# A softplus step with a PSUM operand, its product with x on GpSimd, and new durations in a list scheduler

## The chip, the cores and the metric

The kernel runs on one core of a Trainium2 chip, as one launch. The metric is the device time of that launch in microseconds; lower is better. The core has five engines that run their own instruction queues in order and wait for one another by semaphores: TensorE (matmuls and transposes, PE in the profile, with its weight loads as PEld), VectorE (DVE), ScalarE (ACT), GpSimd (POOL) and SyncE (SP), which here issues nearly all DMAs.

## The reference

Four layers follow one another on an image batch of 8 x 256 x 32 x 32 in float32. Layer 0 is an attention block with a depthwise position term and a feed-forward block with an 8 x 8 Fourier filter; layer 1 is another attention block with group norms; layer 2 is a chain of quantized convolutions that ends in codes of 0 to 255. Layer 3 runs a Mamba block over each image in four directions. The part of it that the change touches is the step size `dt`, which is a softplus, and its product with the convolved and gated input x:

```python
x = jax.nn.silu(xc).swapaxes(1, 2)
x_dbl = x @ W_x.T
dt = jax.nn.softplus(x_dbl[..., :DT_RANK] @ W_dt.T + b_dt)
Bm = x_dbl[..., DT_RANK:DT_RANK + D_STATE]
Cm = x_dbl[..., DT_RANK + D_STATE:]
A = -jnp.exp(A_log)
# for every position of the sequence:
dA = jnp.exp(dt_t[:, :, None] * A)
h = h * dA + dt_t[:, :, None] * B_t[:, None, :] * u_t[:, :, None]
y = jnp.einsum('bdn,bn->bd', h, C_t)
```

There are 512 inner channels, 16 states for each, and 1024 positions; `dt * u` is the product that the change moves.

## The kernel before, in words

**Two phases.** `phase_a` computes layers 0 to 2 for the eight images, each as a strand of generator functions, and stores the codes in DRAM. `phase_b` is the Mamba phase. It goes over 8 images x 4 directions x 2 halves of 512 positions: 64 blocks. A block is 16 groups, one for each state; a group has four channel tiles of 128 channels.

**The order of the work.** Nothing is put in order by hand. Every operation is an `_Op` with an engine and a cost, an estimate of its duration. `_Order.run` is a list scheduler that runs while the program is built: each strand offers its next operation (or list of operations), `start` works out when it could begin from the costs of what has been placed, with 0.35 us for a step from one engine to another, and the one that can begin first is emitted, ties going to the lower rank. So the costs set the order in which each engine's queue is filled; on the chip every queue then runs in that order, and an instruction that has to wait holds up all that is behind it. A strand may give its own cost with a list, as in `yield (SCORES, ops)`. All of the instructions are emitted from one line, L134, which is why the profile's groups are told apart by tiles.

**Fillers.** In `phase_a`, when the list has TensorE idle before an operation, `fill` emits matmuls of a constant into a spare bank (L1077 in the profile), one for each 0.3 us of the planned gap.

**Rooms.** A `_Room` is a set of buffers; `take` waits until one is free and `put` gives it back. Those that matter here, all of `[128, 512]` float32: `dt` (8), `tmp` (3), `xs` (11), `da` (5), `h` (6 pairs) in SBUF, and in PSUM `py` (4 banks, the sums over the states), `db` (3 banks, the scan's input) and `pp`, a single bank. `lend` hands out `pp` to everything beside the scan's own stream: the input projections, the convolution (`conv`), `xdbl`, the softplus steps, the transposes of `du`, the `fold` and the outputs. (Until the first block's softplus steps are done it lends the `py` banks.)

**One group's stream.** ScalarE scales the transposed product by a state's B (`dbu`), TensorE transposes the result into a `db` bank, ScalarE makes the decay `da` as an exponential, VectorE scans (`h`), ScalarE copies the last column (`st`), GpSimd multiplies a pair of scan outputs by C in place (`h<-h,cb`), and TensorE transposes that into the `py` banks, where the sixteen states add up.

**The softplus step.** `steps(n)` makes four strands `dt(c)`, one for each channel tile, which are started during the block before. With v the matmul's result in `pp`, a step computes t = exp(-|v|) on ScalarE, o = max(v, 0) + t on VectorE, then u1 = (t + 1) - 1 on VectorE and ln(1 + t) on ScalarE, and o - u1 + ln(1 + t) on GpSimd. Subtracting (t + 1) - 1 takes back the t that was added with the rounding that 1 + t has. Then o * x goes to u1 on VectorE, TensorE transposes it into `pp` in four pieces, and VectorE copies that to `duT`. The bank `pp` is given back right after o = max(v, 0) + t, and taken anew for the transposes.

Of the kernel before, what the change touches and what calls it, by code (L numbers as in the profile page):

```python
# [20 lines left out]
F32 = mybir.dt.float32  # L21
# [8 lines left out]
P = 128  # L30
# [67 lines left out]
class _Op:  # L98


    def __init__(self, engine, method, args, kw):
        self.engine, self.method, self.args, self.kw = engine, method, args, kw
        out, ins = args[0], [a for a in (*args[1:], *kw.values()) if isinstance(a, bass.AP)]
        self.reads = {k for a in ins for k in self.blocks(a)}
        self.writes = {k for a in (out, kw.get("accum_out")) if a is not None for k in self.blocks(a)}
        self.landing = 0.0
        n = max(math.prod(a.shape[1:]) for a in (out, *ins)) / 1024
        near = all(a.space == out.space and out.space != PSUM for a in ins)
        if engine == "tensor":
            x = kw.get("rhs", ins[0])  # L110
            n = math.prod(x.shape[1:]) / 1024
            move = method == "transpose" or kw.get("is_transpose", False)
            self.cost = max(0.06, n * (0.93 if move else 0.44 if x.dtype != F32 else 1.76 if n > 0.2 else 2.1))
        elif engine == "vector":
            fast = near and method in ("tensor_scalar", "tensor_copy")
            both = near and method == "tensor_tensor"
            scan = method == "tensor_tensor_scan"
            self.cost = 0.04 + n * (2.2 if scan else 0.57 if fast else 1.1) + (0.3 if fast or both else 0)
        elif engine == "scalar":
            self.cost = 0.05 + 0.87 * n + (0.1 if len(ins) > 1 else 0)  # L120
        elif engine == "gpsimd":
            self.cost = 0.13 + 2.17 * n if method == "tensor_tensor" else 0.3 + n
        else:
            self.cost, self.landing = 0.1, 3.0

# [28 lines left out]
class _Room:  # L154
# [6 lines left out]
    def take(self, shape=None, dtype=None):  # L161
        k = self.left.pop(0)
        t = self.pool.tile(shape or self.shape, dtype or self.dtype, name=f"{self.tag}{k}", tag=f"{self.tag}{k}")
        self.of[t.name] = k
        return t

    def put(self, t):
        self.left.append(self.of.pop(t.name))


class _Order:
# [7 lines left out]
    def __init__(self, nc):  # L179
        self.nc, self.strands, self.n = nc, [], 0  # L180
        self.free, self.written, self.read, self.base, self.last = {}, {}, {}, {}, {}
        self.fill = None

    def add(self, rank, strand):
        self.n += 1
# [4 lines left out]
    def go(self, s, value=None):  # L190
        try:
            r = s[1].send(value)
            if isinstance(r, _Op):
                r = (r.cost, [r])
            elif isinstance(r, list):
                r = (sum(o.cost for o in r), r)
            s[2] = r
        except StopIteration:
            self.strands.remove(s)
# [63 lines left out]
def phase_a(ctx, tc, i, col, ident, codes, w_parts):  # L263
# [268 lines left out]
    def maxima(rank, q, k, rows, done):  # L532

        both = yield from take(stats)
        least, sums = both[:, 0], both[:, 1]
        todo = [(t, j, h) for t in range(NT) for j in range(2) for h in (0, 2)]
        left = [MAXIMA]

        def some():
            while todo:  # L540
                yield lambda: not todo or may(2)
                if not todo:
                    break
                n = 4 if may(4) and not todo[0][2] else 2
                t, j, h = todo.pop(0)
                if n == 4 and todo:
                    todo.pop(0)
                bb = yield from some_banks(n)
                ops = []
                for e in range(n):  # L550
                    r = slice(32 * (h + e), 32 * (h + e) + 32)
                    ops.append(
                        T.matmul(bb[e], lhsT=q[r, t * P : (t + 1) * P], rhs=k[r, hs(j)], start=True, stop=True)
                    )
                yield (0.9 if n == 2 else 1.0, ops)
                for e in range(n):
                    m, s = (x[:, j, t, h + e : h + e + 1] for x in (least, sums))
                    yield V.tensor_reduce(m, bb[e], AX.X, ALU.max, negate=True)
                    yield A.activation(bb[e], bb[e], AF.Exp, bias=m, accum_out=s)
                    back(bb[e])  # L560
            left[0] -= 1

        for _ in range(MAXIMA):
            order.add((1, rank), some())
        yield lambda: left[0] == 0 and not making
        making.append(1)
        m, mx, t = (small.tile([P, NT, 4], F32, name=f"mx{e}", tag=f"mx{e}", bufs=2) for e in range(3))
        yield V.tensor_tensor(m, least[:, 0], least[:, 1], ALU.min)
        for j in range(2):
            yield V.tensor_tensor(least[:, j], m, least[:, j], ALU.subtract)  # L570
        yield A.activation(least, least, AF.Exp)
        yield V.tensor_tensor(sums, sums, least, ALU.mult)
        yield V.tensor_tensor(t, sums[:, 0], sums[:, 1], ALU.add)

        y = small.tile([P, NT, 4], F32, name="ln", tag="ln", bufs=2)
        put(stats, both)
        yield A.activation(y, t, AF.Ln)
        yield V.tensor_tensor(mx, y, m, ALU.subtract)
        yield A.activation(y, y, AF.Exp, scale=-1.0)
        yield V.tensor_tensor(t, t, y, ALU.mult)  # L580
        yield V.scalar_tensor_tensor(mx, t, -1.0, mx, ALU.add, ALU.add)
        for e in range(2):
            b = small.tile([P, NT, 4], BF16, name="mb", tag="mb", bufs=2)
            yield V.tensor_copy(b, mx)
            yield V.tensor_copy(parts[:, :, :, e], b)
            yield V.tensor_tensor(mx, mx, parts[:, :, :, e], ALU.subtract)
        yield V.tensor_copy(parts[:, :, :, 2], mx)
        for h in range(2):
            pr = yield from side()
            yield [  # L590
                T.transpose(pr[:, t * P : (t + 1) * P], parts[:, 4 * h + t].rearrange("p a b -> p (a b)"), ident)
                for t in range(4)
            ]
            yield A.copy(rows[:, hs(h)], pr)
            back(pr)
        making.clear()
        done()

    def exponentials(rank, tasks, vt, n, finish):
# [5 lines left out]
        for task, (h, steps) in enumerate(tasks):  # L605
# [31 lines left out]
            def values(k, four, tiles, po=po, seen=seen, last=len(steps) - 1):  # L637
                es = [t[:, e] for t in tiles for e in range(2)]
                yield lambda: seen[0] == k
                ops = []  # L640
                for e, (q, kk, rows, key, r, c, at) in zip(es, four):
                    ops.append(
                        T.matmul(
                            po[at : at + n], lhsT=vt[:, key, c : c + n], rhs=e,
                            start=(k == 0 and key == 0), stop=(k == last), skip_group_check=True,
                        )
                    )
                yield (0.9 * (4 * n // P), ops)
                for t in tiles:
                    put(exps, t)  # L650
                seen[0] += 1
# [403 lines left out]
    def fill(gap, ops):  # L1055
# [6 lines left out]
            [order.last.get((bank.tag, k), 0.0) for k in bank.left] + [order.base.get(o.args[0].name, 0.0)] * own,  # L1062
            default=1e9,
        )
        n = int((gap - max(free, since)) / FILL)
        if n < 1:
            return
        if spare is not None and order.last.get((bank.tag, spare), 0.0) <= since:
# [9 lines left out]
        if t is not None:  # L1078
            bank.put(t)

    order.fill = fill
    stage = [0] * B

    def sample(b):
# [53 lines left out]
def phase_b(ctx, tc, i, col, ident, codes, w_parts, out):  # L1138
# [186 lines left out]
    def steps(n):  # L1325
# [6 lines left out]
        def dt(c):  # L1332
# [1 line left out]
            if c == 0:  # L1334
                d.duT[h] = yield from take(du_room)
            o = yield from take(dt_room)
            t, u1 = yield from takes(2, tmp_room)
            room, ps = yield from lend()
            yield T.matmul(ps, lhsT=w_dt[2 * DS :, c * P : (c + 1) * P], rhs=xd[2 * DS :], start=True, stop=True)
            left[0] -= 1  # L1340
# [4 lines left out]
            yield A.activation(t, ps, AF.Abs)  # L1345
            yield A.activation(t, t, AF.Exp, scale=-1.0)
            yield V.scalar_tensor_tensor(o, ps, 0.0, t, ALU.max, ALU.add)
            put(room, ps)
            yield V.tensor_scalar(u1, t, 1.0, -1.0, ALU.add, ALU.add)
            yield A.activation(t, t, AF.Ln, bias=1.0)  # L1350
            yield G.tensor_tensor(o, o, u1, ALU.subtract)
            yield G.tensor_tensor(o, o, t, ALU.add)
            put(tmp_room, t)
            d.dt[c, h] = o
            yield V.tensor_tensor(u1, o, d.xs[c, h], ALU.mult)
            yield lambda: h in d.duT
            room, pt = yield from lend()
            yield [T.transpose(pt[:, t * P : (t + 1) * P], u1[:, t * P : (t + 1) * P], ident) for t in range(TH)]
            put(tmp_room, u1)
            yield V.tensor_copy(d.duT[h][:, :, c * P : (c + 1) * P], pt.rearrange("p (t k) -> p t k", t=TH))  # L1360
            put(room, pt)
            done.add(("du", c))
# [385 lines left out]
```

## Time and profile before

| | us |
|---|---|
| median of 3 runs | 10703.6 (10692.3 to 10710.17) |
| the profiled execution, its own time | 10710.81 |
| its span, first to last instruction | 10708.9 |
| PE busy | 9899.2 (92%) |
| DVE busy | 8487.3 (79%) |
| ACT busy | 8702.0 (81%) |
| POOL busy | 6736.6 (63%) |

The span lies 1.9 us below the time of the same execution, and that execution 7 us above the median. Busy shares are those of the whole span; the profile's slices show that the first third or so (layers 0 to 2) loads VectorE and GpSimd far less than the Mamba phase does, so each phase has to be read from a window of its own. A row of a group gives the engine, the operation, the tiles written and read, the shapes and the count, then busy time in us, the mean of one in ns, the engine's idle time just before these instructions, and what ended most of it. TensorE's busy time is that of pipelined matmuls with modelled ends and is no measure of work done.

### The profile page before, as it was taken

How to read it: one execution, taken by the hardware profiler on the slowest of the kernel's cores; microseconds unless marked ns; L12 is line 12 of the kernel's file. 1: busy time of each engine (PE TensorE's matmuls, PEld its weight loads, DVE VectorE, ACT ScalarE, POOL GpSimd, SP SyncE). 2: the span in 40 equal slices, each digit the busy share in tenths (PEclk: the TensorE clock that was granted, in tenths of full speed). 3: DMA queues.
4: the chain of work that ended last, by engine and by line, in shares of the span. 5: the costliest groups of instructions: out<-in, count | busy, mean ns of one | idle time of the engine just before them, and what ended most of it. 6: DMA issues, size and time to landing. Idle time of an engine off the chain costs nothing. (4 is left out here: it accounts for less than half of the span.)

```text
span 10708.9 us, 157325 instructions
## 1 busy us (share of the span) xinstructions
PE 9899.2 (92%) x58614; PEld 6251.0 (58%) x58726; DVE 8487.3 (79%) x8991; ACT 8702.0 (81%) x16284; POOL 6736.6 (63%) x3746
## 2 busy tenths in 40 slices
PE   9999999999999899899999999999989999998998
PEld 3333323333333267777777777777777777777776
DVE  5456657577675389888998998998899899899898
ACT  7867676777767488888888988888888888888988
POOL 1532133132220178888888888888888888888888
PEclk8998998999989899999999999999999999999999
DMA  1100000000000011111111111111111111111111
GB/s 53 32 18 16 22 17 22 13 22 13 14 13 10 20 46 41 48 52 47 47 46 52 50 42 56 41 49 52 45 48 52 47 47 46 51 50 43 56 40 50
DMA packets 217346, 410.01 MB, mean 38 GB/s; under 512 B 24881, under 2 KB 69297, under 8 KB 211458
## 3 DMA queue, kind: packets, MB, share of 16 engines
q1 hardware_dynamic: 216578, 399.94, 12.5%
q8 instruction: 461, 7.55, 0.3%
q14 instruction: 307, 2.51, 0.1%
HBM read 358.43 MB, written 30.93 MB: 36 GB/s over the span
## 5 line engine op out<-in xcount | busy, mean ns | idle before, releaser
L134 POOL TENSOR_TENSOR h<-h,cb 128x1024 f32<-128x1024 f32 x2048 | 4874.1, 2394 | 917.3 <-ACT st L134 462.7
L134 ACT ACTIVATE da<-dt,am 128x512 f32<-128x512 f32 x4096 | 2884.7, 717 | 515.6 <-DVE h L134 509.3
L134 DVE TENSOR_TENSOR_SCAN h<-da,st,db 128x512 f32<-128x512 f32 x2048 | 2469.2, 1260 | 177.2 <-PE db L134 96.9
L134 DVE TENSOR_TENSOR_SCAN h<-da,db 128x512 f32<-128x512 f32 x2048 | 2346.4, 1199 | 240.4 <-PE db L134 158.7
L134 ACT ACTIVATE dbu<-du,bT 128x512 f32<-128x512 f32 x3584 | 2487.7, 714 | 30.5 <-PE db L134 28.1
L134 PE MATMUL db<-ident,dbu 128*128 128x128 f32 x14336 | 2218.5, 280 | 169.1 <-DVE h L134 139.6
L134 PE MATMUL py<-ident,h 128*128 128x128 f32 x16384 | 2122.2, 275 | 91.5 <-POOL h L134 83.6
L134 PEld LDWEIGHTS db<-ident,dbu 128*128 128x128 f32 x14336 | 1669.9, 143 | 704.9 <-DVE h L134 377.9
L134 PEld LDWEIGHTS py<-ident,h 128*128 128x128 f32 x16384 | 1843.7, 142 | 168.4 <-POOL h L134 134.0
L134 DVE TENSOR_REDUCE stats<-bank 128x1 f32<-128x512 f32 x1536 | 983.0, 684 | 742.8 <-PE bank L134 741.3
L134 ACT ACTIVATE bank<-bank,stats 128x512 f32<-128x512 f32 x1536 | 1024.5, 672 | 380.9 <-DVE stats L134 370.4
L134 POOL TENSOR_TENSOR mid<-mid,mid 128x961 f32<-128x961 f32 (+2 forms) x192 | 400.3, 2092 | 1056.2 <-ACT mid L134 714.9
L134 PE MATMUL bank<-big,big 32*128 32x512 f32 x4096 | 913.3, 674 | 38.0 <-ACT bank L134 18.7
L134 PE MATMUL pp<-xi,cvd 128*128 128x512 f32 x2016 | 930.6, 605 | 3.5 <-DVE dt L134 1.5
L134 ACT ACTIVATE exps<-bank 128x512 f32<-128x512 f32 x1536 | 797.5, 620 | 135.6 <-PE bank L134 131.2
L134 PE MATMUL db<-dg,du 128*128 128x128 f32 x4096 | 809.0, 280 | 0.0
L134 DVE TENSOR_TENSOR tmp<-dt,xs 128x512 f32<-128x512 f32 x256 | 599.3, 2341 | 173.3 <-POOL dt L134 172.6
L134 POOL TENSOR_TENSOR dt<-dt,tmp 128x512 f32<-128x512 f32 x512 | 653.1, 1276 | 122.6 <-DVE tmp L134 97.5
L134 PEld LDWEIGHTS db<-dg,du 128*128 128x128 f32 x4096 | 636.2, 196 | 0.0
L134 DVE SCALAR_TENSOR_TENSOR mid<-mid,cols,mid 128x961 f32<-128x961 f32 (+1 forms) x384 | 597.2, 1555 | 6.9
L134 PEld LDWEIGHTS pp<-xi,cvd 128*128 128x128 f32 x2016 | 371.9, 195 | 384.3 <-issue 374.2
L134 PEld LDWEIGHTS bank<-big,big 32*128 32x128 f32 x4096 | 285.5, 193 | 503.2 <-issue 253.9
(212 smaller groups left out, 11329.5 us busy)
## 6 DMA issues: line engine op xcount, KB each, us to landing
cb<-c_d SPq DMA_DIRECT2D x1024, 256.0 KB, 3.2
wi<-w_in SPq DMA_DIRECT2D x192, 192.0 KB, 3.5
big<-in_x_dram SPq DMA_DIRECT2D x16, 1024.0 KB, 5.4
kept<-big SPq DMA_DIRECT2D x16, 1024.0 KB, 4.0
big<-kept SPq DMA_DIRECT2D x16, 1024.0 KB, 4.8
cdb<-codes SPq DMA_DIRECT2D x48, 256.0 KB, 4.2
big<-big SPq DMA_DIRECT2D x16, 512.0 KB, 6.7
out_dram<-z SPq DMA_DIRECT2D x32, 256.0 KB, 2.7
```

The source lines that it names most:

```text
L134: return getattr(getattr(nc, self.engine), self.method)(*self.args, **self.kw)
```

## The change

The first part is in the softplus step. The first product of the step, (t + 1) - 1, is written into the PSUM bank that held the matmul's result, VectorE subtracts it from o, and the bank is given back after that. GpSimd only adds ln(1 + t), and it now also does the product with x, into the temporary t; the second temporary u1 is gone.

The second part is in the list scheduler's durations. A matmul whose moving data has fewer than 20 rows costs 0.22 more, a ScalarE operation with a second operand read from memory 0.13 more in place of 0.1, a `tensor_tensor` on GpSimd 0.17 + 2.17 n in place of 0.13 + 2.17 n (n in units of 1024 elements). In `phase_a` alone, every list of TensorE operations without a cost of its own gets 0.1 more (`way`), the list of matmuls in `maxima` is 1.06 whether it has two or four, those of `values` 0.88 for each 128 output rows and 0.12, and `fill` takes 0.35 us off a gap before it counts fillers. In `phase_b` `way` stays at 0.

```diff
-            self.cost = max(0.06, n * (0.93 if move else 0.44 if x.dtype != F32 else 1.76 if n > 0.2 else 2.1))
+            self.cost = max(0.06, (0.22 if x.shape[0] < 20 else 0) + n * (0.93 if move else 0.44 if x.dtype != F32 else 1.76 if n > 0.2 else 2.1))
...
-            self.cost = 0.05 + 0.87 * n + (0.1 if len(ins) > 1 else 0)
+            self.cost = 0.05 + 0.87 * n + (0.13 if len(ins) > 1 else 0)
         elif engine == "gpsimd":
-            self.cost = 0.13 + 2.17 * n if method == "tensor_tensor" else 0.3 + n
+            self.cost = 0.17 + 2.17 * n if method == "tensor_tensor" else 0.3 + n
...
-        self.fill = None
+        self.fill, self.way = None, 0.0
...
-                r = (sum(o.cost for o in r), r)
+                r = (sum(o.cost for o in r) + self.way * (r[0].engine == "tensor"), r)
...
-                yield (0.9 if n == 2 else 1.0, ops)
+                yield (1.06, ops)
...
-                yield (0.9 * (4 * n // P), ops)
+                yield (0.88 * (4 * n // P) + 0.12, ops)
...
-        n = int((gap - max(free, since)) / FILL)
+        n = int((gap - max(free, since) - 0.35) / FILL)
...
-    order.fill = fill
+    order.fill, order.way = fill, 0.1
...
-            t, u1 = yield from takes(2, tmp_room)
+            t = yield from take(tmp_room)
...
             yield V.scalar_tensor_tensor(o, ps, 0.0, t, ALU.max, ALU.add)
+            yield V.tensor_scalar(ps, t, 1.0, -1.0, ALU.add, ALU.add)
+            yield A.activation(t, t, AF.Ln, bias=1.0)
+            yield V.tensor_tensor(o, o, ps, ALU.subtract)
             put(room, ps)
-            yield V.tensor_scalar(u1, t, 1.0, -1.0, ALU.add, ALU.add)
-            yield A.activation(t, t, AF.Ln, bias=1.0)
-            yield G.tensor_tensor(o, o, u1, ALU.subtract)
             yield G.tensor_tensor(o, o, t, ALU.add)
-            put(tmp_room, t)
             d.dt[c, h] = o
-            yield V.tensor_tensor(u1, o, d.xs[c, h], ALU.mult)
+            yield G.tensor_tensor(t, o, d.xs[c, h], ALU.mult)
             yield lambda: h in d.duT
             room, pt = yield from lend()
-            yield [T.transpose(pt[:, t * P : (t + 1) * P], u1[:, t * P : (t + 1) * P], ident) for t in range(TH)]
-            put(tmp_room, u1)
+            yield [T.transpose(pt[:, k * P : (k + 1) * P], t[:, k * P : (k + 1) * P], ident) for k in range(TH)]
+            put(tmp_room, t)
```

## The prediction

> **What bounds the kernel now.** I read the busy shares first, then the scan stretch alone as one window, then the waits in it, then the tile that the change touches. The page's slices show two stages: attention and convolution up to some 3700 us, then the Mamba phase, in which all four engines show 8 or 9 tenths. The window from the first scan to the last (columns: PE, PEld, DVE, ACT, POOL busy):
>
> ```profile
> 3747.00:10663.00 6916.00, 6330.26 (x42789) 4956.78 (x42896) 6223.37 (x5647) 6029.42 (x10493) 5813.06 (x3235) 0.98 0.16 48
> ```
>
> TensorE is busy 91.5%, VectorE 90.0%, ScalarE 87.2%, GpSimd 84.1% of it: no engine is far ahead, so no engine's saved time comes through whole. The waits between 3800 and 10600 us say who holds the others up:
>
> ```profile
> ACT da L134 <- DVE h L134: 501.0, 470, 5.7
> POOL h L134 <- ACT st L134: 437.5, 311, 5.4
> PEld db L134 <- DVE h L134: 370.6, 723, 2.4
> POOL h L134 <- DVE h L134: 268.2, 309, 3.0
> ...
> PE pp L134 <- DVE tmp L134: 195.7, 146, 2.1
> DVE tmp L134 <- POOL dt L134: 170.2, 109, 3.0
> ```
>
> ScalarE waits for scans to give back decay tiles, weight loads wait for scans to give back PSUM banks, GpSimd waits for scan outputs: VectorE is what the rest is late for. VectorE in turn stands 170 us before one instruction, the product with x, and TensorE stands 196 us before the transposes of that product, with all later matmuls queued behind. The tile's own view and the groups show why (minimum/median/maximum ns; busy us, mean ns):
>
> ```profile
> L134 POOL TENSOR_TENSOR dt<-dt,tmp x512: 1262/1274/1645, 3723.7 to 10531.2; 128x512 f32<-128x512 f32 x171
> L134 DVE TENSOR_SCALAR tmp<-tmp x256: 409/694/2589, 3723.2 to 10525.2; 128x512 f32<-128x512 f32 x128
> L134 DVE TENSOR_TENSOR tmp<-dt,xs x256: 660/2599/2852, 3726.7 to 10532.7; 128x512 f32<-128x512 f32 x128
> ...
> L134 DVE TENSOR_TENSOR tmp<-dt,xs 128x512 f32<-128x512 f32 x256 | 599.3, 2341 | 173.3 <-POOL dt L134 172.6
> L134 DVE TENSOR_SCALAR tmp<-tmp 128x512 f32<-128x512 f32 x256 | 289.5, 1131 | 0.1
> L134 DVE TENSOR_TENSOR yT<-py,yT 128x512 f32<-128x512 f32 x64 | 40.2, 672 | 3.6 <-PE py L134 3.6
> ```
>
> The same shape of product takes 660 ns at best and 2599 ns at the median, and the timeline shows what it does in between:
>
> ```profile
> 7015.85 2.35 POOL L134 TENSOR_TENSOR h<-h,cb 128x1024 f32<-128x1024 f32 x1
> ...
> 7015.93 2.83 DVE L134 TENSOR_TENSOR tmp<-dt,xs 128x512 f32<-128x512 f32 x1 [1.90 <-POOL dt L134]
> ```
>
> GpSimd's product began 0.08 us earlier and ended at 7018.20; VectorE's ended at 7018.76, 0.56 us after it. Most of the 2.83 us is standing still.
>
> [...] The trace agrees for a PSUM source (the add of py and yT, 672 ns, never stretched by GpSimd); a PSUM destination from an SBUF source isn't in it.
>
> **The change part by part**, for 256 softplus steps (64 blocks x 4 channel tiles).
>
> *VectorE.* Out go the product (256 x 2341 ns = 599 us) and (t+1)-1 in SBUF (256 x 1131 ns = 290 us), 889 us. In come (t+1)-1 written to the PSUM bank and the subtraction that reads it. For the second I take the 672 ns of the py add. The first is not in the trace: its bounds are 409 ns (the unblocked SBUF form) and 733 ns (the xi scaling from PSUM); I take 0.69 us. 256 x (0.67+0.69) = 348 us. Net 541 us less VectorE work, and the 170 us of standing before the product go too.
>
> *GpSimd.* The subtraction leaves (256 x 1276 ns), the product arrives at the same shape and 1276 ns: zero net. No longer blocked by VectorE's two operations, its long products, 2394 ns mean against 2342 at best, may return up to 2048 x 0.05 = 100 us, on an engine 84% busy; I count none.
>
> *ScalarE, TensorE, DMA.* The same instructions, counts and shapes; no DMA and no queue of SP or POOL issues is touched. The product's transposes read the other temporary. One temporary a step instead of two leaves more of the three free.
>
> *The bank.* All this side work goes through one PSUM bank, pp. Following it in the trace from first matmul to last reader, it is occupied some 4440 us, 64% of the stretch; a softplus step holds it 4.2 us. Now it is given back only after the subtraction: 0.69 + 0.67 us more, and one scan more (1.26 us mean of a scan with carry) where the list puts one while ScalarE takes the logarithm: 1.4 to 2.6 us. 256 x 2.6 = 670 us, occupancy at most 74%. What waits for it is the next matmul into pp, mostly the convolution's, and behind that in TensorE's queue the db and py transposes. I cost it at nothing: the list knows of the hold and puts transposes ahead. If that cover goes, it is the slow rival below.
>
> *What reaches the end in the Mamba phase.* VectorE falls from 90% to (6223-541)/6916 = 82%; TensorE at 91.5% is next, so the gain is what TensorE's idle time of 6916-6330 = 586 us gives back. Of it 196 us is before the product's transposes: the list plans 0.89 us for a product that takes 2.34, so TensorE comes early. On GpSimd the plan (0.17+1.09 = 1.26) meets the 1.28 measured; I give back three quarters, 147 us, the rest being steps where GpSimd is itself late. Before db transposes with scans as cause:
>
> ```profile
> L134 PE MATMUL db<-ident,dbu 128*128 128x128 f32 x14078 | 2178.3, 280 | 165.8 <-DVE h L134 137.3 <-ACT dbu L134 7.3
> ```
>
> Half of 137 us, 69. Before the fold's transposes 28 us wait for VectorE's ys; half, 14. Sum **230 us**, 3.6 us a block of 108.
>
> *The durations.* In the Mamba phase the list gets 0.03 us more for a ScalarE operation with a tile as scale, 0.04 more on GpSimd's products, 0.22 more for the matmul of 17 rows; nothing is added to the machine, orders shift, and I price that inside the 230. In the first phase the new terms move each list of matmuls by about 0.1 us and take 0.35 us off each gap before filler matmuls are counted:
>
> ```profile
> L1077 PE MATMUL bank<-minus 128*128 128x512 bf16 (+1 forms) x1622 | 475.7, 416 | 43.2 <-ACT bank L134 33.9 <-ACT exps L134 6.0 <-POOL eps L316 1.6
> ```
>
> 1622 fillers stand in 445 bursts, 134 of them single. 0.35/0.3 = 1.17 fewer each: 134 + 311 x 1.17 = 498 fewer, at 475.7/1622 = 0.293 us some 146 us of TensorE time. In the attention rounds I read, ScalarE's work (four exponentials, 2.06 us, and two accumulating ones with their reads, 1.8) fills the 3.88 us round, so a filler there hides behind ScalarE. I count a fifth, **30 us**. Bounds: 146 us gained at best; 60 us lost if the new order fits worse or the clock, 0.92 here, falls with fewer fillers (2% of 3300 us).
>
> Against the profiled execution: 10708.9 us span, 10710.8 its own time, 7 us above the median of 10703.6. 10710.8 - 230 - 30 = 10451; set off from the median, **10444 us**.
>
> **The rivals.**
>
> *VectorE's whole gain comes through.* For it: nearly every large wait names VectorE. Against: TensorE 91.5%. If ScalarE (6029 us) then runs at 95%, the stretch is 6029/0.95 = 6346 us, 570 less: with the 30, 10104. Part of the way, 10200. Chance 0.12.
>
> *Nothing moves.* The transposes wait for GpSimd's product as they did for VectorE's, and TensorE's order sets the pace; only the first phase changes: 10690. [...] Chance 0.04.
>
> *Slower: the pp bank blocks TensorE's queue.* The step's hold grows by 2.6 us; in 78% of the steps the next matmul into the bank came within 2 us of the release in the trace. If the list's order doesn't cover it, each step stalls TensorE by 2.6 - 0.9 = 1.7 us: 256 x 1.7 = 435 us, against 260 gained: 10880. It decides where the new stall passes 260/256 = 1.0 us a step. Against it: 36% of the stretch leaves the bank free, and a delayed side job has half a block before it is needed. Chance 0.12.
>
> *As forecast*: chance 0.72, its own range 10310 to 10570.
>
> **How the numbers follow.** The range takes the forecast's range on to half of the large gain and to small gains that the bounds of the PSUM form (256 x 0.3 = 70 us) and of the first phase leave: 10210 to 10670. A measurement here can tell about 0.2%, 21 us. Faster: 0.72 + 0.12 plus a little of the second rival, 0.85; same 0.03; slower 0.12.
>
> **What would show it.** Right: no VectorE row for the product; the PSUM forms near 0.7 us without stretched ones; GpSimd's product at 1.28 us; VectorE near 82% of the stretch; ScalarE's wait for scans well under 501 us; TensorE's wait before the product's transposes near 50 us; some 1100 fillers. Wrong: waits of TensorE for pp's subtraction of over 250 us, transposes waiting for GpSimd's product as long as now, or a first phase more than 60 us longer.

## The result and the profile after

The changed kernel takes **10383.5 us** (median of 4 runs, 10378.2 to 10388.1) against 10706.9 us before: a ratio of 0.9702 with a 95% interval of 0.9687 to 0.9718, 323 us less. The forecast was 10444 us with a range of 10210 to 10670, so the measured time lies inside it and 60 us below the forecast. The first scan starts at 3702 us in place of 3747, the scans take 6639 us in place of 6915, and what follows them 44 in place of 46: 45, 276 and 2 us.

The window from the first scan to the last, of the kernel after (columns as before: PE, PEld, DVE, ACT, POOL busy, then the granted clock):

```profile
3702.00:10341.00 6639.00, 6270.11 (x42898) 4912.56 (x42896) 5716.34 (x5647) 6006.93 (x10493) 5729.03 (x3235) 0.99 0.17 50
```

VectorE's busy time has fallen by 507 us. TensorE, at 94.4%, is the busiest, with ScalarE next at 90.5%; TensorE's idle time went from 586 to 369 us and its busy time from 6330 to 6270. The two add up to the 277 us.

The changed operations in the view of the tile tmp, after (minimum/median/maximum ns):

```profile
L134 POOL TENSOR_TENSOR tmp<-dt,xs x256: 1263/1275/1292, 3683.4 to 10210.7; 128x512 f32<-128x512 f32 x128
...
L134 DVE TENSOR_SCALAR pp<-tmp x252: 694/695/697, 3737.9 to 10206.8; 128x512 f32<-128x512 f32 x126
```

Neither is stretched: the PSUM form spans 3 ns between its fastest and its slowest, where its SBUF form went from 409 to 2589. TensorE's groups in the scan window, with the idle time before them and its causes; two of them before the change:

```profile
L134 PE MATMUL pp<-xi,cvd 128*128 128x512 f32 x2008 | 925.0, 604 | 3.5 <-DVE dt L134 1.5 <-DVE du L134 0.9
...
L134 PE MATMUL pp<-ident,tmp 128*128 128x128 f32 x1008 | 158.8, 280 | 226.9 <-DVE tmp L134 195.7 <-ACT xs L134 15.0 <-ACT dbu L134 9.9
```

and after it:

```profile
L134 PE MATMUL db<-ident,dbu 128*128 128x128 f32 x14334 | 2199.0, 278 | 194.8 <-DVE h L134 168.5 <-ACT dbu L134 10.7
...
L134 PE MATMUL pp<-xi,cvd 128*128 128x512 f32 x2008 | 948.2, 616 | 24.3 <-DVE dt L134 23.8
...
L134 PE MATMUL pp<-ident,tmp 128*128 128x128 f32 x1008 | 154.3, 276 | 17.7 <-ACT xs L134 9.5 <-DVE ys L134 4.1 <-POOL tmp L134 4.1
```

The 227 us before the product's transposes are down to 18. Before the convolution's matmuls TensorE now stands 24 us in place of 3.5, with VectorE's subtraction, which frees the bank, as cause. VectorE's own waits for TensorE, before the change (3800 to 10600 us):

```profile
DVE h L134 <- PE db L134: 242.7, 149, 4.3
...
DVE h L134 <- PE py L134: 70.4, 53, 7.5
```

The waits of the kernel after, 3600 to 10300 us:

```profile
PEld db L134 <- DVE h L134: 414.3, 698, 2.7
DVE h L134 <- PE db L134: 386.4, 308, 5.9
DVE h L134 <- PE py L134: 370.6, 124, 6.5
ACT da L134 <- DVE h L134: 295.0, 422, 4.2
...
ACT xs L134 <- PE pp L134: 169.3, 88, 4.6
...
POOL dt L134 <- DVE dt L134: 145.3, 50, 8.0
```

VectorE, which stood 313 us for TensorE before, now stands 757 us: for a db bank to be filled, and for transposes to free a pair of scan outputs. The others still wait for scans as well: ScalarE 295 us in place of 501, the weight loads 414 in place of 371. Two more waits that grew hang on the bank pp: ScalarE before the convolution's result (64 us before), and GpSimd's add before VectorE's subtraction (before the change GpSimd stood 57 us for (t+1)-1 in that place).

### The profile page after: what moved, and what is told of

It is laid out like the page before. It is cut to its first block, busy times and chain, and to the rows that moved or that the text cites. A ratio compares the mean times of both kernels' runs of the same rounds, so it can differ in the third digit from the quotient of the medians.

```text
span 10385.4 us, 156198 instructions
## 1 busy us (share of the span) xinstructions
PE 9753.1 (94%) x58028; PEld 6225.4 (60%) x58028; DVE 7988.5 (77%) x8997; ACT 8671.1 (83%) x16278; POOL 6635.2 (64%) x3740
## 4 chain that ended last, share of the span: by engine, by line
PE 46%; ACT 25%; DVE 19%; issue 4%; POOL 3%; DMA 2%; SPq 0%; DVEq 0%; POOLq 0%; ACTq 0%
PE bank L134 20%; PE pp L134 10%; ACT da L134 9%; PE py L134 8%; ACT dbu L134 7%; DVE h L134 7%; PE db L134 7%; DVE mid L134 5%; DVE stats L134 2%; POOL h L134 2%; ACT tmp L134 1%; DVE dt L134 1%; ACT xs L134 1%; PE bank L1077 1%; ACT bank L134 1%
## 5 line engine op out<-in xcount | busy, mean ns | idle before, releaser
L134 PE MATMUL py<-ident,h 128*128 128x128 f32 x16384 | 2100.0, 274 | 78.9 <-POOL h L134 59.2
L134 PEld LDWEIGHTS db<-ident,dbu 128*128 128x128 f32 x14336 | 1640.8, 141 | 720.0 <-DVE h L134 422.4
L134 PE MATMUL bank<-big,big 32*128 32x512 f32 x4096 | 960.7, 685 | 42.9 <-ACT bank L134 31.4
L134 PE MATMUL pp<-xi,cvd 128*128 128x512 f32 x2016 | 954.4, 617 | 24.3 <-DVE dt L134 23.8
L134 PEld LDWEIGHTS bank<-big,big 32*128 32x128 f32 x4096 | 331.7, 197 | 529.6 <-issue 206.3
L134 POOL TENSOR_SCALAR big<-big,ga,gs 128x512 f32<-128x512 f32 x64 | 60.9, 967 | 816.6 <-DVE gs L134 479.1
L134 PE MATMUL bank<-exps,big 128*32 128x512 f32 (+1 forms) x3072 | 549.5, 625 | 3.7 <-ACT exps L134 3.7
```

The costliest lines, as they stand in the source:

```text
L134: return getattr(getattr(nc, self.engine), self.method)(*self.args, **self.kw)
```

## The experiments

Times of the scan stretch are read from one trace of each run, first scan to last; ratios are against the kernel before on the same chip.

**The two halves of the change.**

soft_only has the new `dt(c)` and every duration, `way` and `fill` as before; dur_only has the new durations, `way` and `fill`, and `dt(c)` as before.

> The softplus step of the change with all durations of the kernel before. Theory A (VectorE's freed time and the transposes that no longer wait make the gain of the scan stretch): first phase as before, scans from about 3747 us, stretch near 6639 us, in all about 10430 us. Theory B (the new durations of the list make a good part of it): stretch 6750 to 6850 us, in all 10540 to 10640 us.

> The new durations with the softplus step of the kernel before. Theory A: only the first phase gains, about 45 us, the stretch stays within 30 us of 6915: 10660 us. Theory B: the stretch gains 100 to 170 us as well: 10490 to 10560 us. TensorE's wait before the product's transposes stays near 227 us in both, since the product is still priced at 0.89 us on VectorE.

The softplus step alone: 10539 us, ratio 0.9841 (0.9820 to 0.9861). The durations alone: 10621 us, 0.9915 (0.9898 to 0.9932).

| | first scan, us | scan stretch, us |
|---|---|---|
| before | 3747 | 6915 |
| durations alone | 3701 | 6869 |
| softplus alone | 3738 | 6742 |
| both | 3702 | 6639 |

The first phase's 45 us are the durations' alone, give or take a dozen: the first scan starts at 3738 to 3760 us in the three kernels with the old first phase and at 3686 to 3713 in the ten that have the new one whole. In the stretch softplus gives 173 us, the durations 46, and both together 276, 57 more than the sum; why the durations are worth more with the new step wasn't tried. So neither theory held as written: the step alone was to give 276 (A), or 65 to 165 (B), and gave 173. The stretch of the durations alone fell between the two theories as well, and the wait before the product's transposes stayed, at 209 us, as both said.

**The two halves of the softplus change**, both with the new durations. The half that is called the PSUM operand brings three things at once: (t+1)-1 into the bank, the subtraction on VectorE, and one temporary in place of two.

```diff
 psum_only, against the changed kernel:
-            yield G.tensor_tensor(t, o, d.xs[c, h], ALU.mult)
+            yield V.tensor_tensor(t, o, d.xs[c, h], ALU.mult)
 pool_only, against dur_only:
-            yield V.tensor_tensor(u1, o, d.xs[c, h], ALU.mult)
+            yield G.tensor_tensor(u1, o, d.xs[c, h], ALU.mult)
```

> The changed kernel, but the product with x stays on VectorE (same buffers and bank use as the changed kernel). GpSimd is relieved of 256 x 1.28 = 327 us, VectorE has 256 x 2.34 = 599 us more. Theory A: the product is the costly part: its row is stretched to a median near 2.6 us again, TensorE waits some 200 us before its transposes, and the time is 10600 to 10680 us. Rival [...]: 10400 to 10480 us.

> The changed kernel's durations, (t+1)-1 in SBUF and the subtraction on GpSimd as before, but the product on GpSimd. GpSimd has 327 us more than in the changed kernel, 6056 us. Theory A: most of the gain stays, 10430 to 10500 us, with the wait before the product's transposes small. Rival (GpSimd becomes the bound, 91% and more of the stretch): 10600 us or more, with TensorE waiting for GpSimd's h and tmp over 300 us.

The PSUM operand alone: 10663 us, 0.9953 (0.9937 to 0.9969). The product's place alone: **10317 us**, 0.9631 (0.9614 to 0.9648), faster than the whole change and than either theory for it. The rival for psum_only, which had the product's place matter little, named 10400 to 10480 us and is refuted.

| scan stretch, us | product on VectorE | product on GpSimd |
|---|---|---|
| (t+1)-1 in SBUF | 6869 | 6568 |
| (t+1)-1 in PSUM | 6915 | 6639 |

Moving the product gives 301 or 276 us. The PSUM operand costs 46 us in the first column and 71 in the second, though (t+1)-1 is no longer stretched (a mean of 1284 ns in SBUF in the first column and 1071 in the second, 695 in PSUM in both) and, in the first column, 362 us of busy time go off GpSimd. GpSimd as the bound, the rival for pool_only, is refuted by its stretch:

```profile
3706.00:10274.00 6568.00, 6197.76 (x42775) 4884.42 (x42897) 5652.65 (x5395) 6008.07 (x10493) 6071.40 (x3487) 1.00 0.17 50
```

GpSimd is busy 92.4% of it and the kernel is faster. The product of psum_only, on VectorE, is stretched again, a little less than in the kernel before:

```profile
L134 DVE TENSOR_TENSOR tmp<-dt,xs x256: 666/2120/4266, 3681.7 to 10487.5; 128x512 f32<-128x512 f32 x128
```

The time fell where theory A put it, but the wait before the product's transposes is 87 us, not some 200, though the stretch is 46 us longer than that of the durations alone, which has 209. Instead TensorE stands 296 us before its db transposes, against 196 there: this one wait is no measure of what the product's place costs.

**The list or the machine?** If the transposes' wait came from a wrong price in the list, the right price must help with no instruction changed; only the order may.

```diff
-            yield V.tensor_scalar(u1, t, 1.0, -1.0, ALU.add, ALU.add)
+            op = V.tensor_scalar(u1, t, 1.0, -1.0, ALU.add, ALU.add)
+            op.cost = 1.13
+            yield op
...
-            yield V.tensor_tensor(u1, o, d.xs[c, h], ALU.mult)
+            op = V.tensor_tensor(u1, o, d.xs[c, h], ALU.mult)
+            op.cost = 2.34
+            yield op
```

> The kernel before, with the list told the measured prices of the two stretched VectorE operations: 1.13 us for (t+1)-1 and 2.34 us for the product, in place of 0.63 and 0.89. No instruction is added or taken away. Theory M [...]: the stretch stays within 40 us of 6915, 10700 us. Theory P (most of it is that TensorE no longer comes to the transposes early): the wait before the transposes falls from 222 us to under 80 and the stretch by 100 to 170 us: 10530 to 10600 us.

10636 us, 0.9937 (0.9921 to 0.9953). The stretch fell by 76 us, the wait before the transposes from 227 us to about half:

```profile
L134 PE MATMUL pp<-ident,tmp 128*128 128x128 f32 x1008 | 157.0, 279 | 117.7 <-DVE tmp L134 112.4 <-DVE ys L134 2.7 <-ACT dbu L134 2.3
```

Both theories missed, M, which gave the price next to nothing, and P, which gave it most of the gain: it counts, but it is 76 of the 276 us. An operation that takes between 0.66 and 2.85 us has no single right price: the list can be told its mean and no more. pool_true does the same to pool_only, 1.13 in place of 0.63 us for the SBUF form:

> The kernel with the product alone on GpSimd (10317 us), with the list told 1.13 us for (t+1)-1 in SBUF in place of 0.63; no instruction differs. If a wrong price in the list costs as it did in the kernel before (1.95 us a step too low cost 65 us there), half a microsecond a step gives back 15 to 20 us: 10295 to 10305 us. Rival (GpSimd, busy 92% of the stretch, sets the pace): 10310 us or more.

10308 us, 0.9638 (0.9622 to 0.9654), against 0.9631 for pool_only: no difference that these runs can tell. The time lies between what the two theories named.

**The bank's hold.** The changed kernel's step holds pp for a mean of 6.63 us from its first matmul to the end of the subtraction; before it was 4.19. pool_hold keeps the bank longer although its step has no more use for it; tight puts the subtraction in the list right after its operand, so that no scan comes between; tight_hold gives tight's bank back late.

```diff
 pool_hold, against pool_only:
-            put(room, ps)
             yield V.tensor_scalar(u1, t, 1.0, -1.0, ALU.add, ALU.add)
             yield A.activation(t, t, AF.Ln, bias=1.0)
             yield G.tensor_tensor(o, o, u1, ALU.subtract)
+            put(room, ps)
 tight, against the changed kernel:
-            yield A.activation(t, t, AF.Ln, bias=1.0)
             yield V.tensor_tensor(o, o, ps, ALU.subtract)
             put(room, ps)
+            yield A.activation(t, t, AF.Ln, bias=1.0)
 tight_hold, against tight:
-            put(room, ps)
             yield A.activation(t, t, AF.Ln, bias=1.0)
             yield G.tensor_tensor(o, o, t, ALU.add)
+            put(room, ps)
```

> The kernel with the product alone on GpSimd (10317 us), but pp is given back only after GpSimd's subtraction: the bank is held some 3.6 us longer a step, no instruction differs. Theory H (the PSUM operand costs 66 us because of the bank's hold, 2.4 us longer): the stretch grows by 60 to 110 us, 10380 to 10425 us. Rival (it is the subtraction on VectorE or the release of GpSimd that cost it): 10305 to 10330 us.

> The changed kernel with the subtraction offered to the list before the logarithm, so that no scan is put between them and the bank comes free some 1.2 us sooner. Theory H: about half of the 66 us comes back, 10340 to 10365 us, and pp's mean hold falls from 6.6 to 5.4 us. Rival: no effect of the hold, 10375 to 10395 us.

> The kernel with the subtraction ahead of the logarithm (10310 us), but pp is given back only after GpSimd's add, some 3 us later; no instruction differs. Theory H (the bank's hold is the price, in whatever place): 40 to 100 us slower, 10350 to 10410 us. Rival (what tight gained was GpSimd's add no longer waiting for a late subtraction, and the hold as such is hidden): 10300 to 10325 us.

Hold is the mean from the step's first matmul to the end of the operation after which the bank is given back.

| | hold, us | time, us | ratio (interval) | stretch, us |
|---|---|---|---|---|
| pool_only | 4.18 | 10317 | 0.9631 (0.9614 to 0.9648) | 6568 |
| pool_hold | 8.04 | 10420 | 0.9736 (0.9722 to 0.9751) | 6671 |
| changed kernel | 6.63 | 10384 | 0.9702 (0.9687 to 0.9718) | 6639 |
| tight | 5.89 | **10310** | 0.9635 (0.9619 to 0.9651) | 6577 |
| tight_hold | 8.14 | 10456 | 0.9760 (0.9743 to 0.9777) | 6713 |

Holding the bank longer, with the same instructions, costs 103 and 146 us: the hold has a price, through what waits for the bank and through the order that the list then makes, which these runs do not separate. 52 of the 103 us and 44 of the 136 in the stretch are longer busy time of TensorE, whose granted clock is 0.01 lower in both; the rest is idle time. VectorE's waits for TensorE's db transposes, in tight:

```profile
DVE h L134 <- PE db L134: 359.6, 294, 5.3
```

and in tight_hold:

```profile
DVE h L134 <- PE db L134: 481.2, 337, 4.7
```

TensorE in turn stands longer before these transposes; in pool_only and in pool_hold:

```profile
L134 PE MATMUL db<-ident,dbu 128*128 128x128 f32 x14336 | 2181.7, 276 | 135.7 <-DVE h L134 106.5 <-ACT dbu L134 18.7 <-ACT xs L134 0.6
```

```profile
L134 PE MATMUL db<-ident,dbu 128*128 128x128 f32 x14336 | 2206.7, 278 | 234.3 <-DVE h L134 213.2 <-ACT dbu L134 7.7 <-DVE bT L134 0.4
```

A likely reading, not tried by itself, is that the convolution's matmuls come later, among transposes that the scans need, and that VectorE and GpSimd stand behind. The slope isn't one number: of the stretch, 103/3.86 = 27 us go for each us of hold from pool_only to pool_hold, 136/2.25 = 60 from tight to tight_hold. tight shortened the mean hold by 0.74 us, not 1.2, since a scan had stood before the subtraction in only four steps of five, and the time up to o = max(v, 0) + t grew by 0.12 us. It gained more than its theory said: 62 us in the stretch, of which these slopes give 20 to 45. The rest may go with the order that tight changes besides. In the changed kernel GpSimd stood nearly 8 us before an add in fifteen blocks, once in every four. One of them, from the kernel after's timeline (start, duration; in brackets the idle time before):

```profile
4988.49 2.36 POOL L134 TENSOR_TENSOR h<-h,cb 128x1024 f32<-128x1024 f32 x1 [0.65 <-ACT st L134]
...
4990.85 0.69 ACT L134 ACTIVATE xs<-pp,cols 128x512 f32<-128x512 f32 x1 [1.81 <-PE pp L134]
...
4992.07 1.12 PE L134 MATMUL pp<-xd,w_dt 17*128 17x512 f32 x2
...
4994.36 1.22 DVE L134 TENSOR_TENSOR_SCAN h<-da,db 128x512 f32<-128x512 f32 x1 [6.17 <-PE py L134]
...
4998.73 1.28 POOL L134 TENSOR_TENSOR dt<-dt,tmp 128x512 f32<-128x512 f32 x1 [7.88 <-DVE dt L134]
```

The step's matmul came only after ScalarE had emptied pp of a convolution and TensorE had done the matmuls listed in between; GpSimd's add was already at the head of its queue; VectorE meanwhile had no free pair, since TensorE had not come to the transposes that free one. In tight no such wait before an add is left; once the scans run the longest is 4.1 us. soft_only holds the bank for the same 6.63 us and has no such wait either, so it goes with the order that the new durations make and not with the length of the hold alone; what it costs wasn't tried.

**The fillers.**

```diff
-        n = int((gap - max(free, since) - 0.35) / FILL)
+        n = int((gap - max(free, since)) / FILL)
```

> The changed kernel without the 0.35 us taken off a gap before fillers are counted. Theory F (fewer fillers make the first phase's 45 us): fillers rise from 924 by 400 or more, the first scan starts 25 to 45 us later, 10410 to 10430 us. Rival (the lists' new durations make it): within 12 us of 10383, and the clock, if anything, higher than 0.90.

10387 us, 0.9705 (0.9691 to 0.9720): no difference. 1376 fillers in place of 924, and the first scan starts at 3693 us, within the 3686 to 3713 us of the ten runs that have the new first phase whole. The 452 more fillers add 128 us of TensorE's time, and yet it is busy 3449 us up to 3702 us with them and 3450 without: the granted clock was 0.93 with them and 0.90 without, and the other matmuls took that much less. The two cancel here. So the 45 us come from the other new durations of the first phase; which of them wasn't tried.

**Further on from tight.**

```diff
 early_ln, against tight: the logarithm into a second temporary, right after Exp
+            yield A.activation(u, t, AF.Ln, bias=1.0)
...
 tight_da6, against tight:
-    da_room = _Room(rooms, "da", 5, [P, HALF])
-    tmp_room = _Room(rooms, "tmp", 3, [P, HALF])
+    da_room = _Room(rooms, "da", 6, [P, HALF])
+    tmp_room = _Room(rooms, "tmp", 2, [P, HALF])
```

> As tight, but the logarithm goes to a second temporary right after the exponential, so that it waits for no VectorE operation and GpSimd's add waits for the subtraction alone. Two temporaries a step again. If the 79 us in which GpSimd's add waits for ScalarE count: 10270 to 10300 us. Rival (the stretch is set by TensorE, and the first temporary is missed): 10305 to 10330 us.

> As tight, with one of the three temporaries, of which a step now needs one, given to the decay room: tmp 2, da 6. If ScalarE's wait for scans to free decay tiles (283 us) is on the path: it falls below 200 us and the time to 10260 to 10295 us. Rival (ScalarE runs ahead only to wait elsewhere, or two temporaries are too few): 10300 us or more.

early_ln takes 10314 us (0.9625, 0.9611 to 0.9640) and tight_da6 10318 us (0.9628, 0.9614 to 0.9642). Neither differs from tight. With a sixth decay tile ScalarE waits for scans 283 us, as with five: one more tile did not shorten that wait. That early_ln's second temporary costs nothing also says that the number of temporaries isn't what the PSUM half pays for. Five kernels, pool_only, pool_true, tight and these two, end within 11 us of one another, 65 to 76 us ahead of the change.

## Why the prediction was right, and where not

*VectorE's sum* held. 0.69 us was taken for the PSUM form and 0.67 for the subtraction; 0.695 and 0.666 were measured. That the PSUM form would not be stretched was the author's estimate: the trace before shows it for a PSUM source alone, the add of py and yT, 658 to 692 ns in 64 cases, 29 of them beside a long product (`h<-h,cb`) of GpSimd. 541 us were to go, 507 went, the difference lying in overlaps and in scans slower by 3 to 4 ns each. The 170 us before the product are gone with it. VectorE's share of the stretch is 86% and not the 82% that was given as a sign, since VectorE lost 34 us less and the stretch itself became shorter.

*GpSimd at zero* held: its long products' busy time fell by 47 us, less than the 100 allowed, and at 92% in pool_only it did not become the bound. In the kernel before, 112 of the 2048 took over 2.44 us, up to 2.85, and each of these began while VectorE ran the product or (t+1)-1; in the kernel after the longest takes 2.44.

*What reaches the end* had nearly the right total from wrong terms, and that was in part luck. TensorE's idle time gave back 217 us against the 230 of the sum, mainly in this way: before the transposes 209 (147 forecast), before the fold's transposes 29 (14), before the db transposes a loss of 26 (69 gained, by the forecast), and 21 lost before the convolution (nothing was forecast). The failed term is the db one, and it goes with the hold of the bank: with the product moved and the hold short, in pool_only, this idle time is 136 us, 33 less than the 169 before; in the changed kernel it is 195, in pool_hold 234. And 60 us came from TensorE's busy time, which the sum took as fixed; with them the stretch gave 276 us. Its reason for the wait before the transposes, the list's price of the product, held for half of it: told the right price, true_prices kept 118 of the 227 us. The two misses of the sum, 95 us too much at db and 62 too little before the product's transposes, nearly cancelled with the smaller ones.

*The bank at nothing* is the step that failed. The hold was sized rightly, 1.4 to 2.6 us more by the forecast and 2.44 measured, and so was the bank's occupancy, at most 74% by the forecast and 73% in the trace. That "the list knows of the hold and puts transposes ahead" is not enough: the PSUM half costs 46 to 71 us by the four-cell table, and tight, which keeps it and shortens the hold, gets 62 of them back. The slow rival thus named the right mechanism at too large a price, 1.7 us a step where 71/256 = 0.28 us was paid, and far below its threshold of 1.0.

*The stretching* can be read closely from the trace. In the kernel before, 230 of the 256 products took over 1 us; each of them began while GpSimd ran a long product (`h<-h,cb`) and ended 0.54 to 0.56 us after it. So did the 110 of the (t+1)-1 in SBUF that took over 1 us, ending 0.28 to 0.29 us after it. The form with a PSUM operand took 694 to 697 ns in all 252 cases, 213 of them beside a long product, and was yet the half of the change that lost. pool_only leaves (t+1)-1 stretched, at a mean of 1071 ns, and is faster.

*The first phase*: 45 us against 30, from the wrong cause. The 30 were a fifth of the fillers' time; fewer fillers are worth nothing here, and the lists' new durations, which were priced only as a risk, made the gain. 924 fillers were left, not some 1100.

*The list's prices in the Mamba phase* were "priced inside the 230" without a term of their own. They gave 46 us alone, and 103 once the step was changed (6742 to 6639).

## What to carry to other kernels

When an instruction is stretched by another engine, try it on the engine that held it up, even if that one is nearly as busy: here 1.28 us there, planned to within 0.02, was worth more than a mean of 2.34 us that varied between 0.7 and 2.9. A scratch operand in a bank that is handed round among several users is paid in time held: put what ends the hold close behind what begins it, and test by giving the bank back late, which adds no instruction, though the list's order moves with it. Price an idle engine's gain by what it waits for next, not by what it waits for now.

## What the runs showed of the hardware that was not expected

TensorE's granted clock in the scan stretch differs between kernels with the same matmuls: 0.98 with 6330 us busy and 586 idle (before), 0.99 with 6270 and 369 (after), 1.00 with 6198 and 370 (pool_only). Of these three the one with the most idle time has the lowest clock, but idle time summed over the stretch doesn't order the clocks of all runs: soft_only has 0.98 with 416 us idle, dur_only 0.99 with 549. One hundredth of 6270 us is 63 us, the size of the 60 and 72 us of busy time between the first three, so part of the gain may be TensorE running faster. tight_hold speaks against so simple a sum, busy 6274 us at 0.98, as long as the changed kernel at 0.99. This is read from windows with two digits of clock, and what sets it here stays open.

In the kernel before, all 230 products on VectorE that took over 1 us ended 0.54 to 0.56 us after the long product of GpSimd beside which they began, and all 110 such `tensor_scalar` 0.28 to 0.29 us after it; the profile shows the whole wait as busy time of VectorE. A VectorE operation from SBUF to PSUM (128 x 512, float32, two immediates) took 694 to 697 ns in all 252 cases of the kernel after, beside a GpSimd that was 86% busy.
